# Two graph-convolution layers: part of each block's weights made directly behind the previous block's application, and several waits placed elsewhere

## The chip, the cores and the metric

The kernel runs on one core of a Trainium2 chip. The metric is the device time of one execution in microseconds (us). Smaller is better. The engines are named as in the profile: PE is TensorE's matrix multiplication, PEld its weight load, DVE is VectorE, ACT is ScalarE, POOL is GpSimd and SP is SyncE; the last two mostly start DMA transfers.

## What is computed

The input x has 8 batches of 2048 nodes with 64 features; adj is a 2048 x 2048 matrix. Two layers follow each other, each with a residual and a layer norm:

```
# layer 0: K = 3 supports I, A, 2A@A - I;  weights of each node from its embedding
w   = einsum('nd,dkio->nkio', embedding, weight);  b = einsum('nd,do->no', embedding, bias)
x_g = einsum('knm,bmc->bnkc', A_stack, x)
x   = layernorm(x + einsum('bnki,nkio->bno', x_g, w) + b)
# layer 1: the same with supports I, A, 2A@A - I and softmax(relu(E @ E.T))
x   = layernorm(x + einsum('bnki,nkio->bno', x_g, weights) + bias)
```

Every node has its own 64 x 64 weight matrix for each support. It is never held for all nodes: it is made for one block of 256 nodes, used there, and overwritten.

## The kernel before

**Stages.** The 2048 nodes are cut into 8 blocks of 256. The work is five phases of 8 stages, one stage per block: A0 (stages 0 to 7: layer 0, product of adj with x), B0 (8 to 15: layer 0, second product), A1 (16 to 23: layer 1, first product, and the row statistics of the softmax), Z1 (24 to 31: layer 1, product with the softmax matrix) and V1 (32 to 39: layer 1, second product of adj). Stages 26 to 31 work in pairs ("wide"). Block 0 of A0, B0, A1 and V1, block 1 of A0, and blocks 0 and 1 of Z1 use plain products; the other blocks use a seven-product (Strassen) scheme.

**The main product** of a stage is a Python generator that emits one matmul after another and reports its progress in units of the stage's length (64 for plain blocks, 56 for Strassen blocks). `put(n, place, job)` hangs a job on stage n at a place from 0 to 64, scaled to the length; as soon as the progress has reached the place, the job's instructions are emitted. `spread` puts several jobs at even distances. All instructions are kept in this program order on their engine's queue. So a place in this list is a position in every engine's queue, and an instruction that waits holds up all that stand behind it on its engine.

**The jobs that matter here:**

- `weights(g0, g1)` makes groups g0 to g1 - 1 of a block's node weights. There are 16 groups in A0, A1 and V1. A group is four matmuls `pw<-e,wst` (of 64 rows, two side by side) into one PSUM buffer, and one copy of 128 x 1024 values from it to `w`, on ACT or DVE. `cuts` says which groups go in one job. The jobs of stage n are hung on stage n + 1 (A0, A1) or on stage n itself (V1).
- `apply(c)` multiplies one quarter of a block with its weights (`po<-w,t`) into one PSUM buffer; DVE adds it into `acc` with four instructions. The four calls of a block follow each other in a "burst" on the next stage.
- `post` finishes a block of B0 or V1: the layer norm, in three parts (mean and squares; variance; scaling and store). For B0 the store goes to `x1d` in DRAM, and `load_x` brings it back as X for layer 1.
- `repeat` copies half of the transposed features `t` to the other half by a DMA (`t<-t`), which B0's applications need.
- `bias` makes a block's bias (`pb<-bst,e`) and adds it to x on DVE (`bx`).
- `load_e` loads a block's embedding into one of two tiles `e2` by POOL's queue (and in Z1 also `c`, the softmax constants).
- `numerators` and `scores` (`ps<-e,s`) make the softmax matrix, `scores_of_rows` (`pr`) its row statistics, `turn` (`pt`) transposes.

**Buffers.** `pw`, `po`, `pb`, `pt`, `ps` and `pr` all take the next one of three PSUM buffers of 4 KB per partition (pool `ps_big`, `bufs=3`); each waits until the tile three places ahead of it has been read out. The main products use two accumulators (`ps_acc`, `bufs=2`): the seven products p1, p4, p7, p2, p6, p5, p3 take them in turn, so p3 needs what p6 used.

The lines of the plan that are touched are 776 (`cuts`), 784 to 794 (B0), 818 (`bias`), 827 (`load` of `load_e` in Z1), and line 331 (which engine copies a group).

Of the kernel before, what the change touches and what calls it, by code (L numbers as in the profile page):

```python
# [24 lines left out]
SB = NB // P  # L25
# [4 lines left out]
V1 = C // 4  # L30
# [18 lines left out]
def two_graph_layers(ctx: ExitStack, tc: tile.TileContext, x, x_t, adj_b, adj_q, layers, out):  # L49
# [40 lines left out]
    def big(name):  # L90
        return ps_big.tile([P, 2, 512], F32, tag="big", name=name)

    def copy(i, dst, src):

        if i % 2:
            act.activation(dst, src, AF.Copy)
        else:
            dve.tensor_copy(dst, src)
# [42 lines left out]
    ps = big("pi")  # L141
# [120 lines left out]
    class Stage:  # L262
# [50 lines left out]
        def weights(self, g0, g1):  # L313
            if g0 == 0:
                self.w = w_room[:, 0:NB * self.units].rearrange("p (n o) -> p n o", n=NB)
            made = []
            for g in range(g0, g1):
                if g % 4 == 0:
                    self.ws = wst.next()
                ps = big("pw").rearrange("p h (v n) -> p h v n", n=NB)  # L320
                for i in range(2):
                    for h in range(2):
                        r = slice(64 * h, 64 * h + 64)
                        pe.matmul(ps[:, h, i, :], self.ws[r, 2 * (g % 4) + i, :], self.e2[r, :],
                                  start=True, stop=True)
                made.append(ps)
            if g1 == self.units // 4:
                wst.fill()
            for g, ps in zip(range(g0, g1), made):
                dst = self.w[:, :, 4 * g:4 * g + 4].rearrange("p n (v h) -> p n v h", h=2)  # L330
                copy(0 if g % (8 if self.phase == "A0" else 3) == 1 else 1, dst, ps.rearrange("p h v n -> p n v h"))


        def apply(self, c):
# [405 lines left out]
    def put(n, i, f, *args):  # L740
        plans[n].setdefault(i * stages[n].length / 64, []).append((f, args))

    def spread(n, first, last, jobs):
        for i, job in enumerate(jobs):
            put(n, first + (last - first) * i / max(len(jobs) - 1, 1), *job)
# [28 lines left out]
    for n, st in enumerate(stages):  # L774
        phase = st.phase
        cuts = (0, 3, 6, 9, 12, 14, 16) if st.units == C else (0, 3, 6, 8)
        weights = [(st.weights, *g) for g in zip(cuts, cuts[1:])]
        bursts = None
        if phase == "A0":
            for c in range(NJ // 4 if st.j == 1 else 0):  # L780
                put(n, 16 * c + 10, st.sums_of_a, c)
            spread(n + 1, 1, 31, weights)
            turned, bursts, posts = 33, (38, 38, 38, 38), (50,)
        elif phase == "B0":
            if st.j == 7:
                spread(n, 40, 60, weights)
                bursts, posts = (6, 6, 12, 12), ()
                put(n + 1, 26, st.load_x, range(SB))
                for k in range(6):
                    put(n + 1, (13 if k < 3 else 14) + 2 * k, st.post, k % 3, 8 - k // 3 * 8, 16 - k // 3 * 8)  # L790
            else:
                spread(n + 1, 3, 13, weights)
                bursts, posts = (19, 19, 29, 29), (38, 42, 48)
                put(n + 2, 5, st.load_x, range(SB))
        elif phase == "A1":
            spread(n + 1, 12, 36, weights)
            turned, bursts, posts = 4, (43, 43, 43, 43), (56,)
            for s, h, place in ((0, 0, 38), (0, 1, 40), (1, 0, 57), (1, 1, 60)):
                put(n, place, st.scores_of_rows, s, h)
            put(n, 41, st.statistics, 0)  # L800
            put(*((n, 62) if st.j else (n + 1, 6)), st.statistics, 1)
            put(n + 1, 24, st.store_c)
        elif phase == "V1":
            spread(n, (22 if st.j else 4), (62 if st.j < 7 else 52), weights)
            bursts, posts = (4, 4, 4, 4), (15, 19, 23)
            put(n, 20, st.load_z)
        if bursts and n + 1 < len(stages):
            if phase[0] == "A":
                put(n + 1, turned, st.turn, 1)
            for i, place in enumerate(bursts):  # L810
                put(n + 1, place, st.apply, i if phase == "A0" else i ^ 2)
            for k, place in enumerate(posts):
                put(n + 1, place, st.post, k)
        if n + 1 < len(stages):
            if n < 25 or n > 30:
                put(n, 44 if n < 23 else 37 if n < 25 else 4, stages[n + 1].load_e)
        if phase[0] == "A":
            put(*((1, 12) if n == 0 else (n, 28) if st.li == 0 else (n, 37)), st.bias)
            if st.li == 0:
                put(max(n, 1), 20 if n else 4, st.load_xt)  # L820
            else:
                put(n, 47 if st.j else 57, st.turn, 0, "x")
        if phase != "Z1":
            put(*((1, 26) if n == 0 else (n, 48 + 6 * st.li) if st.kk == 0 else (n, 30)), st.load_acc)
        elif st.wide:
            first, even, odd = (n - 2, (16, 24, 32), (40, 48, 56)) if n % 2 == 0 else (n - 2, (28, 36, 44), (4, 12, 20))
            load = (n - 2, 4) if n % 2 == 0 else (n - 3, 20)
            if n == 26:
                first, even, odd, load = 25, (4, 10, 18), (20, 26, 34), (24, 40)
            elif n == 27:  # L830
                first, even, odd, load = 25, (56, 61, 67), (42, 48, 54), (25, 33)
            put(*load, st.load_e)
            for t, places in enumerate((even, odd)):
                for i, place in enumerate(places):
                    at = (first, place) if place < 64 else (first + 1, place - 64)
                    put(*at, *((st.numerators, t, i) if i < 2 else (st.normalize, t)))
        else:
            st.p = [None] * 8
            for c in range(8):
                if c < 3:  # L840
                    put(n - 1, (50, 54, 62)[c] if n < 26 else 40 + 8 * c, st.scores, c)
                else:
                    put(n, 8 * (c - 3), st.scores, c)
# [71 lines left out]
```

## Time and profile before

| | |
|---|---|
| time, median of 3 runs | 1491.45 us (1489.88 to 1492.27) |
| the profiled execution: its own time | 1492.28 us |
| its span, first to last instruction | 1490.5 us |
| mean granted TensorE clock | 0.993 |
| PE busy, share of the span | 1453.0 us, 97% |
| DVE busy | 954.6 us, 64% |
| ACT busy | 474.1 us, 32% |
| POOL busy | 207.4 us, 14% |

The profile page has a line for each engine's busy time, the span in 40 slices, and the chain of work that ended last. The trace behind it can be asked for the instructions in order of time ("timeline"). A timeline line gives the start in us, the duration in us, the engine, the program line (nearly always that of a helper, L43), the operation with its tiles, how often it was repeated, and in square brackets the idle time before it and what ended it. The trace counts each fp32 matmul of the program as two instructions, and the `pw`, `pb`, `pr` and `ps` matmuls as one.

### The profile page before, as it was taken

To read this page: it belongs to the slowest core of one execution; us is meant where nothing else is said; L and a number is where in the kernel's file an instruction comes from. 1 tells how busy PE (TensorE), PEld (TensorE's weight loads), DVE (VectorE), ACT (ScalarE), POOL (GpSimd) and SP (SyncE) were. 2 spreads that over 40 slices of the span, in tenths; PEclk is the share of its full clock that TensorE was granted. 3 is DMA by queue.
4 is the path that set the end of the run, shared out by engine and by line. 5 is a ranking of instruction groups with operands and counts; after the bars stand their busy time and mean duration, and the time that the engine had idled before them with its cause. 6 is when DMAs were issued, how large, how long until landed. Compare 5 with 4: busy or idle time off the path is not lost.

```text
span 1490.5 us, 31130 instructions
## 1 busy us (share of the span) xinstructions
PE 1453.0 (97%) x13310; PEld 1182.8 (79%) x13310; DVE 954.6 (64%) x1614; ACT 474.1 (32%) x590; POOL 207.4 (14%) x343
## 2 busy tenths in 40 slices
PE   9899999999999999899999999999999999999996
PEld 4467777778989989467777777788888888888885
DVE  3876666637666666766666667567794466666665
ACT  1344444432211212064444444432120233333332
POOL 4222221210111111111011111101100000000100
PEclk9999999999999999999999999999999999999998
DMA  9788898884656666578777787212313656666551
GB/s 360 251 280 264 276 282 267 267 317 154 203 189 202 202 197 204 157 177 186 195 192 175 198 209 208 50 40 66 90 43 112 206 180 193 192 190 194 190 194 51
DMA packets 86730, 283.37 MB, mean 190 GB/s; under 512 B 14016, under 2 KB 18112, under 8 KB 84992
## 3 DMA queue, kind: packets, MB, share of 16 engines
q1 hardware_dynamic: 53600, 171.99, 38.5%
q0 software_dynamic: 27520, 95.76, 21.2%
q10 hardware_dynamic: 5472, 13.63, 2.9%
q8 instruction: 105, 1.72, 0.5%
q14 instruction: 33, 0.27, 0.1%
HBM read 216.28 MB, written 60.83 MB: 186 GB/s over the span
## 4 chain that ended last, share of the span: by engine, by line
PE 70%; issue 20%; DVE 3%; POOL 3%; DMA 3%; ACT 1%; POOLq 0%; ACTq 0%; DVEq 0%
PE p L43 40%; PE po L43 11%; PE pw L43 8%; PE pz L43 6%; PE pu L43 2%; PE pt L43 1%; DMA x<-in_x 1%; DVE w L43 1%; PE pr L43 1%; DVE acc L43 1%; PE ps L43 1%; POOL e L43 1%; POOL x1d L43 1%; DMA u<-in_w 1%; POOL t L43 1%
## 5 line engine op out<-in xcount | busy, mean ns | idle before, releaser
L43 ACT ACTIVATE w<-pw 128x1024 f32<-128x1024 f32 x328 | 318.5, 1021 | 391.6 <-PE pw L43 388.9
L43 DVE SCALAR_TENSOR_TENSOR acc<-po,mask,acc 128x256 f32<-128x256 f32 (+1 forms) x640 | 247.0, 426 | 82.7 <-PE po L43 70.0
L43 DVE COPY w<-pw 128x1024 f32<-128x1024 f32 x120 | 146.9, 1224 | 140.7 <-PE pw L43 139.4
L43 PE MATMUL p<-a,u 128*128 128x128 f32 x1792 | 219.4, 278 | 4.4 <-PE p L43 4.1
L43 PEld LDWEIGHTS p<-a,u 128*128 128x128 f32 x1792 | 206.6, 192 | 15.2 <-PE p L43 5.1
L43 PE MATMUL po<-w,t 128*32 128x256 f32 (+1 forms) x5120 | 206.1, 337 | 6.1 <-issue 5.0
L43 PE MATMUL p<-u,a 128*128 128x256 f32 x832 | 203.6, 387 | 0.0
L43 PEld LDWEIGHTS po<-w,t 128*32 128x32 f32 (+1 forms) x5120 | 125.9, 108 | 80.0 <-issue 14.0
L43 PEld LDWEIGHTS p<-u,a 128*128 128x128 f32 x832 | 152.0, 190 | 29.7 <-issue 5.4
L43 PE MATMUL p<-x,a 128*128 128x256 f32 x624 | 152.6, 385 | 0.0
L43 PE MATMUL pw<-e,wst 64*128 64x256 f32 x1728 | 146.0, 296 | 1.2 <-ACT w L43 1.1
L43 PEld LDWEIGHTS pw<-e,wst 64*128 64x128 f32 x1728 | 112.1, 184 | 41.8 <-issue 21.6
L43 PEld LDWEIGHTS p<-x,a 128*128 128x128 f32 x624 | 114.2, 190 | 19.0 <-issue 0.7
L43 PE MATMUL pu<-x,a 128*128 128x512 f32 x192 | 90.5, 617 | 3.6 <-DMA x<-x1d 2.1
L43 PE MATMUL p<-w,u 128*128 128x256 f32 x384 | 87.5, 384 | 0.0
L43 PE MATMUL p<-a,x 128*128 128x128 f32 x672 | 82.9, 278 | 0.0
L43 PE MATMUL p<-a,w 128*128 128x128 f32 x672 | 81.3, 277 | 0.0
L43 PEld LDWEIGHTS p<-w,u 128*128 128x128 f32 x384 | 73.2, 193 | 9.8
L43 PEld LDWEIGHTS p<-a,x 128*128 128x128 f32 x672 | 77.7, 192 | 2.8
L43 PEld LDWEIGHTS p<-a,w 128*128 128x128 f32 x672 | 77.3, 192 | 2.5 <-issue 1.4
L43 DVE TENSOR_TENSOR temps<-p,temps 128x256 f32<-128x256 f32 x108 | 43.1, 420 | 44.4 <-PE p L43 43.7
L43 PEld LDWEIGHTS pu<-x,a 128*128 128x128 f32 x192 | 35.5, 193 | 45.1 <-issue 36.1
(122 smaller groups left out, 1413.8 us busy)
## 6 DMA issues: line engine op xcount, KB each, us to landing
wst<-wd SPq DMA_DIRECT2D x108, 512.0 KB, 6.5
a<-in_adj_q SPq DMA_DIRECT2D x87, 512.0 KB, 5.2
a<-sd SPq DMA_DIRECT2D x84, 512.0 KB, 4.2
sd<-a POOLq DMA_DIRECT2D x24, 512.0 KB, 6.4
a<-in_adj_b SPq DMA_DIRECT2D x16, 512.0 KB, 6.5
bx<-bx POOLq DMA_DIRECT2D x32, 256.0 KB, 6.7
acc<-bx POOLq DMA_DIRECT2D x16, 512.0 KB, 6.1
pd<-acc POOLq DMA_DIRECT2D x16, 512.0 KB, 5.0
```

Of the source, the lines that this page charges most:

```text
L43: return self._tc.keep_in_program_order(f(*args, **kwargs))
```

## The change

The first group of weights of blocks 1 to 7 in A0, A1 and V1 is made directly behind the last call of the previous block's application (places 38, 43 and 4), and the other 15 groups follow in five jobs of three instead of the earlier six jobs for 16 groups. In A0 the copies that go to DVE are groups 2 and 10 instead of 1 and 9, and none for stage 0. The bias of stage 0 moves from stage 1, place 12, to stage 0, place 28. In B0 parts 1 and 2 of the norm move from places 42 and 48 to 46.5 and 50. The last application of layer 0 (block 7 of B0, in stage 16) moves from places 6 and 12 to 0 and 6, with its norm parts and `load_x` 6 places earlier. In Z1 the embedding loads of stages 28 to 31 move: 28 from (26, 4) to (25, 40), 29 from (26, 20) to (26, 8), 30 from (28, 4) to (27, 4), 31 from (28, 20) to (28, 8).

```diff
-                copy(0 if g % (8 if self.phase == "A0" else 3) == 1 else 1, dst, ps.rearrange("p h v n -> p n v h"))
+                copy(0 if self.n and g % (8 if self.phase == "A0" else 3) == (2 if self.phase == "A0" else 1) else 1, dst, ps.rearrange("p h v n -> p n v h"))
...
         cuts = (0, 3, 6, 9, 12, 14, 16) if st.units == C else (0, 3, 6, 8)
+        behind = {"A0": 38, "A1": 43, "V1": 4}.get(phase) if st.j else None
+        if behind:
+            put(n, behind, st.weights, 0, 1)
+            cuts = (1, 4, 7, 10, 13, 16)
         weights = [(st.weights, *g) for g in zip(cuts, cuts[1:])]
...
             if st.j == 7:
                 spread(n, 40, 60, weights)
-                bursts, posts = (6, 6, 12, 12), ()
-                put(n + 1, 26, st.load_x, range(SB))
+                bursts, posts = (0, 0, 6, 6), ()
+                put(n + 1, 20, st.load_x, range(SB))
                 for k in range(6):
-                    put(n + 1, (13 if k < 3 else 14) + 2 * k, st.post, k % 3, 8 - k // 3 * 8, 16 - k // 3 * 8)
+                    put(n + 1, (7 if k < 3 else 8) + 2 * k, st.post, k % 3, 8 - k // 3 * 8, 16 - k // 3 * 8)
             else:
                 spread(n + 1, 3, 13, weights)
-                bursts, posts = (19, 19, 29, 29), (38, 42, 48)
+                bursts, posts = (19, 19, 29, 29), (38, 46.5, 50)
...
-            put(*((1, 12) if n == 0 else (n, 28) if st.li == 0 else (n, 37)), st.bias)
+            put(*((n, 28) if st.li == 0 else (n, 37)), st.bias)
...
-            load = (n - 2, 4) if n % 2 == 0 else (n - 3, 20)
+            load = ((25, 40) if n == 28 else (n - 3, 4)) if n % 2 == 0 else (n - 3, 8)
```

## The prediction

> **What bounds the kernel now.** First the page: busy time, then the chain.
>
> ```profile
> PE 1453.0 (97%) x13310; PEld 1182.8 (79%) x13310; DVE 954.6 (64%) x1614; ACT 474.1 (32%) x590; POOL 207.4 (14%) x343
> ...
> PE 70%; issue 20%; DVE 3%; POOL 3%; DMA 3%; ACT 1%; POOLq 0%; ACTq 0%; DVEq 0%
> ```
>
> TensorE is the bound: every gap in its queue ends up in the time, and other engines count only where it waits for them. So I read its timeline for waits (idle time and its releaser in brackets).
>
> ```profile
> 40.22 0.72 PE L43 MATMUL pw<-e,wsplit 64*128 64x256 f32 x8 [1.36 <-DVE w L43]
> 47.01 0.51 PE L43 MATMUL pw<-e,wsplit 64*128 64x256 f32 x4 [2.41 <-DVE bx L43]
> ...
> 488.66 5.15 PE L43 MATMUL p<-a,u 128*128 128x128 f32 x44 [0.69 <-PE p L43]
> ...
> 602.24 2.01 PE L43 MATMUL po<-w,t 64*32 64x128 f32 x126 [1.12 <-DMA t<-t]
> ...
> 630.30 1.12 PE L43 MATMUL pu<-x,a 128*128 128x512 f32 x2 [1.97 <-DMA x<-x1d]
> ...
> 1016.42 0.71 PE L43 MATMUL ps<-e,s 128*128 128x256 f32 x4 [2.00 <-DMA e<-ed]
> 1071.98 0.71 PE L43 MATMUL ps<-e,s 128*128 128x256 f32 x4 [1.50 <-DMA e<-ed]
> ```
>
> Each stands where the change moves something. Then the windows view behind three of them (PEclk is the column before the DMA share):
>
> ```profile
> 632.00:636.00 4.00, 4.00 (x11) 2.01 (x10) 3.86 (x12) 1.84 (x2) 2.09 (x4) 0.57 0.47 164
> 1017.50:1021.50 4.00, 4.00 (x14) 3.18 (x12) 3.81 (x3) 1.53 (x2) 0.00 (x0) 0.57 0.04 14
> 48.00:51.50 3.50, 3.50 (x6) 1.10 (x4) 1.07 (x1) 0.58 (x1) 1.83 (x4) 0.57 1.02 290
> ```
>
> Each time the clock is halved for 3.41 us, so 1.7 us are lost. Start to start, matmuls of 128, 256 and 512 columns cost 112, 216 and 429 ns in the undisturbed streams; what exceeds this is the loss used below.
>
> [...]
>
> **The change, part by part.**
>
> *First group behind the application.* Weights jobs of 12 matmuls take 905 ns, of 8 665: 60 ns each and 181 fixed. The neighbouring products are 92 ns late before and 104 after: 377 ns per interruption. One interruption in each of 21 stages (7 each in A0, A1, V1) goes; in its place comes a change from `po` (128 x 32) to `pw` (64 x 128). No trace row shows it; bounds are 0 and the 270 ns (92 + 181) that `pw` costs out of a product. I take 200: gain about 0.17 us (0.1 to 0.37), x21 = **-3.6** (-2 to -7.7). The buffer it asks for was `po` number two's: DVE starts on A1's block at 709.28 and needs 7.89 / 4 = 1.97 us a tile, so 713.2, while TensorE asks at 714.3. No wait; A0 and V1 likewise have 1.0 us. ACT's copy (1.02 us) lies in idle ACT time: 9 us in A1 and V1, 17 us in A0.
>
> *The five jobs of three.* Each fills all three PSUM buffers, and whoever comes next waits for the first group's copy. In A1 that is the bias, one matmul behind the last job:
>
> ```profile
> 702.68 0.73 PE L43 MATMUL pw<-e,wst 64*128 64x256 f32 x8
> 703.34 0.70 PE L43 MATMUL p<-u,a 128*128 128x256 f32 x2
> 703.69 0.49 PE L43 MATMUL pb<-bst,e 128*128 128x64 f32 x2
> ```
>
> Now this job has groups 13, 14, 15, and 13 goes to DVE (13 modulo 3 is 1). Job start + 0.55 (from such jobs' first copies) + 1.22 copy + 0.06 = 1.83; `pb` asks at 0.905 + 0.35 = 1.25. Wait 0.58, in stages 18 to 23: **+3.5**. In A0 the transposes ask at 1.44 and ACT frees the buffer at 0.60 + 1.02 + 0.06 = 1.68: 0.24 in stages 2 to 7, **+1.4**. In stage 24 `ps` stands right behind a job: 1.83 - 0.905 = **+0.9**. V1 has nothing close behind.
>
> *B0's norm parts.* At 487.8 p3 waits for p6's buffer, because DVE runs the variance (1.22 us, and 1.18 waiting for ACT's squares) ahead of p6's sums. At 46.5 it comes after them (p6 ends at 40 of 56, place 45.7). Excess over cadence 0.80 to 0.87 us in stages 9 to 14: **-5.1**. Next latest: p5's sums, about 0.65 us ahead of their need.
>
> *Stage 0's bias.* At place 28 TensorE has done 28 rows of `pu`, at about 18.2 us, and meets `pb`, which needs the embedding:
>
> ```profile
> 14.75 20.01 PE L43 MATMUL pu<-x,a 128*128 128x512 f32 x46 [0.35 <-DMA x<-in_x]
> ...
> 17.78 1.16 POOL L43 DMA_DIRECT2D e<-ed x2
> ...
> DMA to landing us min/median/max: 5.6/5.7/6.0
> ```
>
> The second transfer starts at 18.36 and lands at 24.1: a wait of 5.9, then half clock, 1.7 (0.9 to 2.6). Behind it on DVE, `bx` pushes the splits 1.1 us, which TensorE no longer feels. POOL issues `bx` ahead of the next embedding (20.6 to about 27), needed only near 60. In stage 1 the waits go: 1.6 (copies all on ACT, 3 x 0.97 us per 3.5), 2.67 (`bx`), 1.66 of clock. **+1.7** (0.5 to 3).
>
> *Layer 0's last application.* TensorE gets to it at 598.05. `t<-t` is issued at 596.10 and landed 6.1 later, at 602.2. Before, six `pu` rows covered part. Now it waits 4.2, and 1.5 of clock follow. The second pair meets the second copy (599.40, landed 7.5 later) as before. Posts: DVE's start is unchanged, but the scaling is no longer behind a 2.02 us sum, so X lands at about 629.1; TensorE, 2.6 us of matmuls behind, asks at 631.6. Gone: 1.4, 2.1 and 1.7. 4.2 + 1.5 - 5.2 = **+0.6** (-1.5 to +3).
>
> *Z1's loads.* Stage 28's stood on POOL behind `zd<-t`, which waited for DVE until 1011.06. At (25, 40) it goes once stage 26's `c` is free, about 996; need 1014. Stage 30's gains a stage. Excesses 2.17 and 1.66, clock 1.7: **-5.5** (-3.8 without the clock). Stages 29 and 31 had no wait: nothing. POOL passes the loads ahead of stores needed a phase later.
>
> *Nothing:* groups 2 and 10 for 1 and 9 in A0 keep DVE's work the same.
>
> **Sum:** -3.6 + 3.5 + 1.4 + 0.9 - 5.1 + 1.7 + 0.6 - 5.5 = -6.1 against the profiled 1492.28 (span 1490.5 and 1.8 around it): 1486.2. That execution is 0.8 above the median[...]. I say 1486. A difference under 0.2% (3 us) can't be told from none.
>
> **Rivals.**
>
> *Less: no difference (16%).* [...]the group at 270 (+1.5), Z1's clock gain absent (+1.7): -0.9, 1491. [...]Against: all three must coincide.
>
> *More (13%).* The three-job waits (5.8 together) don't appear, because the copies start earlier than 0.55: -11.9, 1480. Against: start and copy were measured on many jobs.
>
> *Slower (12%).* The group behind the application waits for DVE. It asks 1.0 us after its buffer comes free. If DVE's drain is 1.0 + d late, 21 stages lose d each; from d = 0.43 (9.1 / 21) the kernel is over 0.2% slower; d = 0.7 gives 1501. For: in A0 DVE enters the burst straight from other work (144.56, a tenth late). Against: `po` shows no wait on DVE there. That the change doesn't do what it says is no rival: queue order follows the plan.
>
> Faster holds the rest: 72%, same 16, slower 12. The likeliest case alone is 1482 to 1490; for 8 in 10 I take 1479 to 1492.5, which adds the rivals' near ends.
>
> **To look for after:** a wait of about 6 us on `e<-ed` near 18 us; 4 us on `t<-t` near 600; `pw` x4 behind `po` without a wait; no p3 gaps in B0; 0.6 us before `pb` in A1; none at `ps` near 1010 and 1065. A `pw` wait behind `po`, or A1 without its `pb` wait, would make me wrong.

## The result and the profile after

The changed kernel took 1493.99 us (median; 1493.32 to 1494.92), the kernel before in the runs beside it 1490.66 (1488.69 to 1492.27): a ratio of 1.0023, 95% interval 1.0006 to 1.0041. The forecast was 1486.0 and faster; it became slower by about 3 us. The profiled executions lie closer together than the medians: 1492.28 before (at the top of its range) and 1493.32 after (at the bottom of its own), spans 1490.5 and 1491.6.

The page of the changed kernel, busy time and chain:

```profile
PE 1450.4 (97%) x13310; PEld 1185.0 (79%) x13310; DVE 953.4 (64%) x1612; ACT 476.9 (32%) x592; POOL 206.8 (14%) x343
...
PE 53%; DMA 1%; DVE 1%; issue 1%; ACT 1%; ACTq 0%
```

Nothing has changed hands: TensorE has the same work and is still the bound. (The second line's shares of the chain add up to only 57% of the span, so the chain is no guide here.) So again the waits in TensorE's timeline decide, here at the places that the prediction listed (the last column is the idle time before the line and what ended it):

```profile
25.11 0.61 PE L43 MATMUL pb<-bst,e 128*128 128x64 f32 x2 [6.95 <-DMA e<-ed]
43.87 0.97 PE L43 MATMUL pw<-e,wsplit 64*128 64x256 f32 x12
...
485.78 3.74 PE L43 MATMUL p<-a,w 128*128 128x128 f32 x32
489.35 5.08 PE L43 MATMUL p<-a,u 128*128 128x128 f32 x44
...
603.12 3.41 PE L43 MATMUL po<-w,t 64*32 64x128 f32 x126 [5.31 <-DMA t<-t]
...
644.12 1.97 PE L43 MATMUL pt<-ident,u 128*128 128x128 f32 x8 [2.62 <-ACT u L43]
...
1013.97 0.82 PE L43 MATMUL ps<-e,s 128*128 128x256 f32 x4
1073.91 0.83 PE L43 MATMUL ps<-e,s 128*128 128x256 f32 x4
```

Stage 1's weights, p3 in B0 and Z1's `ps` have lost their brackets, as forecast. The embedding and `t<-t` are waited for, as forecast, but for longer. The wait of `pt` on ACT is new and was not forecast. The windows view shows the clock (0.50 in the column before the DMA share) at half rate behind all three waits:

```profile
22.50:29.00 6.50, 3.89 (x6) 1.94 (x7) 3.17 (x5) 1.28 (x1) 2.23 (x4) 0.50 1.05 380
602.80:606.00 3.20, 2.88 (x112) 2.88 (x119) 0.83 (x4) 0.00 (x0) 0.00 (x0) 0.50 1.01 206
643.80:647.00 3.20, 2.88 (x11) 2.71 (x12) 0.00 (x0) 1.13 (x3) 0.00 (x0) 0.50 0.63 194
```

**Where the time went.** Each block's application is a burst of `po` on TensorE. The differences between the starts of these bursts cut the span into pieces that can be compared between all kernels. The columns: *start* is the time of the first burst; *A0* and *A1* run from their first block's burst to their last; *B0* over its first seven blocks; *16* from B0's seventh burst to A1's first, so layer 0's last application and what follows; *Z1* from A1's last block's burst to V1's first; *V1* from there to the second half of the very last application. The piece between A0 and B0 is 29.5 us in every kernel, and what follows the last column 19.0 to 19.4. Each row is one execution.

| kernel (us, profiled execution) | start | A0 | B0 | 16 | A1 | Z1 | V1 |
|---|---|---|---|---|---|---|---|
| before | 63.5 | 273.6 | 205.3 | 94.0 | 292.8 | 243.3 | 269.1 |
| changed | 66.5 | 275.2 | 200.0 | 98.4 | 296.9 | 237.5 | 268.5 |
| stage 16 put back | 66.3 | 275.2 | 199.9 | 99.0 | 295.9 | 237.5 | 268.1 |
| stage 0's bias at 48 | 57.3 | 275.2 | 200.0 | 101.1 | 297.5 | 237.5 | 267.8 |
| other bias places | 67.5 | 274.4 | 199.6 | 99.7 | 293.2 | 237.5 | 267.8 |
| old cuts | 66.3 | 273.6 | 199.9 | 99.9 | 292.9 | 237.5 | 269.1 |
| late refill | 67.5 | 276.8 | 200.6 | 97.0 | 296.4 | 237.5 | 267.8 |
| before + norm parts | 63.8 | 273.6 | 199.9 | 98.9 | 292.9 | 241.4 | 269.1 |
| before + norm parts + late refill | 62.2 | 273.6 | 199.3 | 94.2 | 292.8 | 241.9 | 269.1 |
| before + Z1's loads | 61.9 | 273.6 | 204.5 | 94.7 | 293.2 | 237.5 | 269.1 |
| combined | 60.3 | 273.6 | 200.0 | 92.6 | 292.8 | 237.5 | 268.2 |

Forecast against measured, by piece (the forecast is the sum of the prediction's own terms): start +1.7 against +3.0; A0 +0.2 against +1.5; B0 -5.1 against -5.3; stage 16 +0.6 against +4.4; A1 +3.2 against +4.0; Z1 -5.5 against -5.8; V1 -1.2 against -0.6. That is -6.1 against +1.3. Half of the miss, 3.8 of 7.4, is stage 16.

### The profile page after: what moved, and what is told of

It reads as the page before. It is cut to its first block, busy times and chain, and to the rows that moved or that the text cites. A ratio compares the mean times of both kernels' runs of the same rounds, so it can differ in the third digit from the quotient of the medians.

```text
span 1491.6 us, 31148 instructions
## 1 busy us (share of the span) xinstructions
PE 1450.4 (97%) x13310; PEld 1185.0 (79%) x13310; DVE 953.4 (64%) x1612; ACT 476.9 (32%) x592; POOL 206.8 (14%) x343
## 4 chain that ended last, share of the span: by engine, by line
PE 53%; DMA 1%; DVE 1%; issue 1%; ACT 1%; ACTq 0%
PE p L43 32%; PE po L43 7%; PE pz L43 6%; PE pw L43 5%; DMA wst<-wd 1%; PE ps L43 1%; PE pt L43 1%; PE pr L43 1%; DVE w L43 1%; DVE acc L43 0%; PE pb L43 0%; ACT row L43 0%; ACT t L43 0%; ACT sq L43 0%; ACT w L43 0%
## 5 line engine op out<-in xcount | busy, mean ns | idle before, releaser
L43 ACT ACTIVATE sq<-acc 128x1024 f32<-128x1024 f32 (+2 forms) x19 | 17.5, 922 | 166.5 <-DVE acc L43 153.9
```

Source lines behind the costliest of these rows:

```text
L43: return self._tc.keep_in_program_order(f(*args, **kwargs))
```

## The experiments

The kernels are measured against the kernel before, run beside them on the same chip; times are medians.

**1. Stage 16 put back.** The obvious suspect first.

```diff
-                bursts, posts = (0, 0, 6, 6), ()
-                put(n + 1, 20, st.load_x, range(SB))
+                bursts, posts = (6, 6, 12, 12), ()
+                put(n + 1, 26, st.load_x, range(SB))
-                    put(n + 1, (7 if k < 3 else 8) + 2 * k, st.post, k % 3, 8 - k // 3 * 8, 16 - k // 3 * 8)
+                    put(n + 1, (13 if k < 3 else 14) + 2 * k, st.post, k % 3, 8 - k // 3 * 8, 16 - k // 3 * 8)
```

> The changed kernel with layer 0's last application (stage 16) at its old places: bursts (6, 6, 12, 12), posts at 13/14, load_x at 26; all else as changed. Theory (the early application cost TensorE 5.3 us of waiting on t<-t and, by emptying the queue, uncovered the chain DVE sums - statistics - ACT table load - u copy, 2.6 us more, plus two halved clock stretches): the stretch from stage 15's to stage 17's application is about 4.5 us shorter than in the changed kernel's profile (offset there from -0.8 to +3.7), with po waiting 1.1 on t<-t and pu 2.0 on X again, and no wait of pt on ACT. Whole time -4 to -4.5 against the changed kernel. Rival (only the landing time of that one DMA was unlucky, 7.3 instead of 6.1, and the rest would have come out equal): the stretch is 1.2 us shorter at most.

Measured: 1493.95 us, ratio 1.0019 (1.0009 to 1.0029). Stage 16 took 99.0 us, not less than the 98.4 with the change. The theory fell: with the application back at its old place TensorE still waited 3.5 us for `t<-t` (1.1 before), 2.8 for X and 2.0 for ACT's `u`. Something else in the change had made `t<-t` late: 8.1 us from its issue to the application, 6.1 before.

**2. Stage 0's bias at place 48.**

```diff
-            put(*((n, 28) if st.li == 0 else (n, 37)), st.bias)
+            put(*((0, 48) if n == 0 else (n, 28) if st.li == 0 else (n, 37)), st.bias)
```

> The changed kernel with only stage 0's bias moved from place 28 to place 48 of stage 0, where its embedding has landed (25.0 us in the changed kernel's profile; TensorE gets to place 48 near 27). Theory (the wait of 6.95 us on e<-ed and the 1.8 us of half clock are lost only because of the place): no wait in stage 0 and none back in stage 1, since bx (1.3 us) ends long before the first weights; stage 0 is 8.5 to 8.8 us shorter than in the changed kernel. Rival (the embedding's arrival or bx's place in DVE's queue, between the splits of 2.5 us, costs it again a little later, as pw<-DVE bx near 45): only 3 to 5 us shorter.

Measured: 1486.38 us, ratio 0.9972 (0.9959 to 0.9985). The first application came at 57.3 instead of 66.5, 9.2 us earlier, and 6.2 earlier than in the kernel before. `pb` stood at 26.24 with no wait, and the first weights at 34.68 without one. The theory held; the place alone cost it.

**3. Other bias places in A0 and A1.**

```diff
-            put(*((n, 28) if st.li == 0 else (n, 37)), st.bias)
+            put(*((0, 28) if n == 0 else (n, 26) if st.li == 0 else (n, 33)), st.bias)
```

> The changed kernel with only the biases of stages 1 to 7 and 16 to 23 moved: A0 from place 28 to 26, A1 from 37 to 33, so that pb and its bx are not next to the last job of three groups. Theory (one cause for both losses: with three groups in a row all three PSUM buffers are taken, and the bias's buffer is one of the three): A0's last jobs are 905 instead of 1410 to 1460 ns long, 0.47 less in each of stages 2 to 7; in A1 the 0.39 ahead of pb goes in stages 18 to 23, with at most 0.07 of it back ahead of pr. Sum -4.6 to -5.2. Rival (the copies as such are late, since more of them go behind one another on DVE, whatever stands next): the wait moves to pr in A1 and to pt in A0, sum 0 to -1.

Measured: 1490.41 us, ratio 0.9993 (0.9981 to 1.0006). A1's piece lost 3.6 us, A0's only 0.8. The changed kernel first, in A0: the timeline of a stage's end.

```profile
178.13 0.49 PE L43 MATMUL pb<-bst,e 128*128 128x64 f32 x2
...
180.90 0.51 PE L43 MATMUL pw<-e,wst 64*128 64x256 f32 x4 [0.23 <-DVE bx L43]
181.33 0.70 PE L43 MATMUL p<-x,a 128*128 128x256 f32 x2
181.87 0.82 PE L43 MATMUL pt<-ident,u 128*128 128x128 f32 x6
```

The job's third group asks for the buffer of the bias, three places ahead of it, and DVE reads that only at 179.47 to 180.75. From the job's start at 179.93 to the next product matmul it is 1.40 us instead of 0.905. The transposes then follow 0.54 us behind the product matmul, as usual. With the bias moved:

```profile
180.78 0.97 PE L43 MATMUL pw<-e,wst 64*128 64x256 f32 x12
181.68 0.70 PE L43 MATMUL p<-x,a 128*128 128x256 f32 x2
182.46 0.76 PE L43 MATMUL pt<-ident,u 128*128 128x128 f32 x5
```

The job is 0.90 us long again, and now the transposes come 0.78 behind the product matmul: 0.24 late, the very wait that the prediction had for this place. It had been there all along, behind a longer one. So in A0 the rival (the wait moves to `pt`) was right by half; in A1 the theory held.

**4. Old cuts.** The lines of `behind` and `cuts` taken out; groups 1 and 9 on DVE in A0, none in stage 0.

> The changed kernel without the group behind the application: old cuts (0, 3, 6, 9, 12, 14, 16), groups 1 and 9 on DVE in A0 (none in stage 0); all else as changed. Theory (the group behind the application saves 0.19 us per stage, and its jobs of three lose 0.47 in A0 and 0.49 in A1 at the bias): against the changed kernel's profile stages 2 to 7 -0.28 each, A1's -0.29 each, stage 24 -0.8, V1's +0.19 each: sum about -1.7 -1.7 -0.8 +1.3 = -2.9. Rival (the group behind the application is itself late, so that its removal brings more in every phase, V1 too): V1's stages shorter as well, sum -4 and beyond.

Measured: 1489.69 us, ratio 0.9984 (0.9971 to 0.9997). The steps of A0 fell by 0.28 and those of A1 by 0.29 each, stage 24 by 0.8, and V1's rose by 0.17 to 0.21: the theory, stage by stage. A0, A1 and V1 together gave 4.9 instead of 2.9, as two waits in A1 for the refill of `wst` (stages 18 and 23, 0.5 and 1.0) and a gap of 0.6 in V1 went as well; the whole execution shows 3.8, since stage 16 took 1.4 more in this one. V1 shows the gain of the group behind the application directly. In A0 and A1 it is what is left once the waits behind the jobs of three are taken off, and these waits cost more than it brings.

**5. Late refill.** What made `t<-t` late? In the trace two transfers stand close together: POOL's `t<-t`, and SP's refill of `wst` that stage 15's last weights job releases. The DMA issues of the kernel before, of the changed kernel, and of the kernel before with the norm parts alone (number 6), in this order (SPq is SP's queue):

```profile
596.10 0.53 POOL L43 DMA_DIRECT2D t<-t  x1 [0.86 <-DVE t L43]
596.52 0.33 SPq L43 DMA_DIRECT2D wst<-wd  x1
```

```profile
595.79 0.33 SPq L43 DMA_DIRECT2D wst<-wd  x1
595.82 0.53 POOL L43 DMA_DIRECT2D t<-t  x1 [0.85 <-DVE t L43]
```

```profile
591.58 0.33 SPq L43 DMA_DIRECT2D wst<-wd  x1
591.59 0.53 POOL L43 DMA_DIRECT2D t<-t  x1 [0.86 <-DVE t L43]
```

Before, the copy was issued 0.42 us ahead of the refill; since, just behind it. The edit moves the refill back:

```diff
-                spread(n, 40, 60, weights)
+                spread(n, 40, 50, weights[:2])
+                put(n, 63, *weights[2])
```

> The changed kernel with only the last weights job of stage 15 moved from place 60 to 63 (about 0.8 us later), so that the refill of wst (512 KB on SP's queue) that it releases is issued behind the first t<-t instead of 0.03 us ahead of it. In the kernel before, t<-t was issued 0.42 us ahead of that refill, and the application followed 6.1 us after its issue; in the changed kernel and the four kernels built on it the refill went 0.02 to 0.17 us ahead, and it took 7.3 to 9.0 us. Theory (the norm parts' move takes p3's stalls out of B0, TensorE ends its weights job earlier against DVE, and so the refill goes ahead of t<-t through the same DMA engines): the application follows 6.0 to 6.4 us after the issue, the wait at po is 4.2 to 4.6. Rival (chance, or the store x1d<-acc 2.1 us ahead of t<-t in every kernel): 7.3 us or more, as in the other five.

Measured: 1491.66 us, ratio 0.9994 (0.9985 to 1.0004). The application followed 5.4 us after the issue, and `po` waited 2.3 us for the copy, behind 1.0 for a weights copy that the later job itself delays. Stage 16 took 97.0 us, where the changed kernel took 98.4 and the four built on it without this edit 99.0 to 101.1.

**6. The norm parts alone**, on the kernel before: `posts` (38, 46.5, 50) instead of (38, 42, 48).

> The kernel before with one part of the change: B0's norm parts at (38, 46.5, 50). Theory: up to stage 15's application -5.3 as forecast (waits of p3 gone), and then a price that the forecast did not see: the wst refill goes ahead of t<-t, which lands 7.3 to 9 us after its issue instead of 6.1. The six pu rows cover 2.8 of it, so the wait at po grows from 1.1 to 2.5 to 4.2 us, and an idle time over 2 us can halve the clock (1.7 more); X and the rest follow that chain. Whole time against before: -5.3 +1.5 to +4.5, that is -1 to -4. Rival (the landing time has nothing to do with the norm parts): wait at po 1.0 to 1.5, whole time -5.3.

Measured: 1490.29 us, ratio 0.9989 (0.9977 to 1.0000). B0 gave 5.3 us and stage 16 took 4.9 back. Its timeline:

```profile
595.79 0.40 PE L43 MATMUL po<-w,t 64*32 64x128 f32 x2
599.64 3.66 PE L43 MATMUL po<-w,t 64*32 64x128 f32 x126 [3.45 <-DMA t<-t]
```

The application stands at its old place, and yet waits 3.45 us instead of 1.12. The 126 matmuls took 3.66 us instead of 2.01 and the six of `pu` behind them 3.62 instead of 2.84, 2.4 us more together: the times of a halved clock, as in the changed kernel, where the same 126 took 3.41 at a clock of 0.50.

The DMA view shows how the two queues shared the 16 DMA engines. In the fourth us after the issue of `t<-t`, SP's queue took 87% of their time in the changed kernel and POOL's queue 11%; in the kernel before it was 38% for SP and 46% for POOL.

**7. The norm parts with the late refill**, on the kernel before: the edits of 6 and 5 together.

> The kernel before with two edits: B0's norm parts at (38, 46.5, 50), and stage 15's last weights job at 63 instead of 60. With the norm parts alone t<-t went 0.01 us behind the refill of wst, the application followed 8.0 us after its issue, and stage 16 gave back 4.9 of the 5.3 us. Theory (order of t<-t and the refill on the DMA engines): the application follows 5.4 to 6.5 us after t<-t's issue, as in the three runs with the late job; po waits 0 to 1.2 us without a halved clock, stages 15 and 16 together take at most 94.5 us (94.0 before, 98.9 with the norm parts alone), and the whole is -4 to -6 against before. Rival (it is the kernel around it, not the order): 98 us again and -0.5 to -2.

Measured: 1485.21 us, ratio 0.9956 (0.9940 to 0.9973). Stage 16 took 94.2 us.

```profile
589.14 0.53 POOL L43 DMA_DIRECT2D t<-t  x1 [0.85 <-DVE t L43]
590.46 0.33 SPq L43 DMA_DIRECT2D wst<-wd  x1
...
594.79 2.01 PE L43 MATMUL po<-w,t 64*32 64x128 f32 x126 [1.07 <-DMA t<-t]
```

The copy is ahead of the refill again, lands in time, and the wait is 1.07. One place of one job, and the same norm parts give 7 us instead of 2. So what experiment 1 left open is the refill: issued behind the copy, here by 1.3 us, it no longer delays it. (Z1's column in numbers 6 and 7 is 1.5 to 1.9 lower than before although nothing was edited there. Before, the clock was halved for 3.41 us behind a wait for the embedding of 2.00, which cost 1.7; here the longest of these waits were 1.9 and 2.0. That the clock was not halved behind them would fit the column, but was not shown.)

**8. Z1's loads alone**, on the kernel before: only the `load` line.

> The kernel before with one part of the change: Z1's embedding loads. Theory: the waits of ps on e<-ed near 1016 and 1072 (2.2 and 1.7 above cadence) and the halved clock behind the first (1.7) go, -5.5 to -5.8 in Z1, nothing elsewhere. Rival (the loads, now ahead of zd and other stores on POOL's queue, hold those up, or e comes too early and waits for its tile's release): a new wait in Z1 and -3 or less.

Measured: 1489.22 us, ratio 0.9978 (0.9962 to 0.9993). Z1 gave 5.80 us, as in the changed kernel, and no wait took their place. The profiled execution was the fastest of this kernel; by the medians the whole is 3.9 faster.

**9. Combined.** The parts that gained, without those that lost. Stage 0's bias at (0, 48), the late refill, old cuts in A0 and A1 and `behind` for V1 alone, norm parts and Z1's loads as changed, and a new order in stage 16:

```diff
-        behind = {"A0": 38, "A1": 43, "V1": 4}.get(phase) if st.j else None
+        behind = {"V1": 4}.get(phase) if st.j else None
...
-                bursts, posts = (0, 0, 6, 6), ()
-                put(n + 1, 20, st.load_x, range(SB))
+                bursts, posts = (9, 9, 14, 14), ()
+                put(n + 1, 23, st.load_x, range(SB))
-                    put(n + 1, (7 if k < 3 else 8) + 2 * k, st.post, k % 3, 8 - k // 3 * 8, 16 - k // 3 * 8)
+                    put(n + 1, 15 + k, st.post, k % 3, 8 - k // 3 * 8, 16 - k // 3 * 8)
...
-        put(16, 24 + 4 * i, sums["A1"].make, i, 0, 7)
-        put(16, 50, sums["A1"].make, i, 7, 8)
+        put(16, 24 + 4 * i if i < 2 else 42, sums["A1"].make, i, 0, 7)
+        put(17, 2, sums["A1"].make, i, 7, 8)
```

> The parts of the change that gained, without those that lost: B0's norm parts and Z1's loads as changed; the group behind the application in V1 only (A0 and A1 with the old cuts); stage 0's bias at (0, 48), with stage 0's groups all on ACT; stage 15's last weights job at 63; and stage 16 in a new order: bursts (9, 9, 14, 14), norm parts at 15 to 20, load_x at 23, two of the four A1 sums for blocks 0 to 6 behind the first row statistics (place 42 instead of 32 and 36), and the sums' last eighth at (17, 2) instead of (16, 50). Expected against before: start -5.8, B0 -5.3, Z1 -5.8, V1 -1.3, stage 16 -3 to -6 (no wait at po over 1 us, no halved clock; pt's wait on ACT gone because the statistics no longer stand behind 10 us of sums): about -21 to -24, near 1468. Rival (stage 16's chain of t<-t, application, norm and x1d is one length whatever the order, so its waits only move to pu<-X or pt): stage 16 gives 0 to -1, near 1472.

Measured: 1474.97 us, ratio 0.9883 (0.9863 to 0.9904): faster than both kernels, by less than expected. The start gave 3.2 instead of 5.8, as `pt` in stage 1 waited 1.5 us for that stage's bias and `po` behind it another 0.8. Stage 16 gave 1.4: `po` waited 0.36 and `pt` no longer, but TensorE now reaches X 2.63 us too early, and the clock is halved behind that wait (4.58 us for six matmuls that took 2.84 behind `po` in the kernel before):

```profile
594.36 2.01 PE L43 MATMUL po<-w,t 64*32 64x128 f32 x126 [0.36 <-DMA t<-t]
620.89 4.58 PE L43 MATMUL pu<-x,a 128*128 128x512 f32 x6 [2.63 <-DMA x<-x1d]
```

The rival was nearer the mark there.

**10. Combined, with the sums as before.** It tells what `pt`'s wait on ACT hangs on.

> As the combined kernel, but all four A1 sums at their old places (16, 24 to 36) and the last eighth at (16, 50). It tells apart what pt<-ACT u hangs on. Theory (ten us of sums on DVE hold up the row statistics, these the exponentials on ACT, these the copy of u): pt waits 4 to 7 us on ACT's u copy (2.6 in the changed kernel, where TensorE came 5 to 7 us later), and the whole is 3 to 6 us slower than the combined kernel. Rival (pt's wait came from the clock or from X): within 1 us of the combined kernel.

Measured: 1476.56 us, ratio 0.9895 (0.9874 to 0.9916). From the second pair of applications to A1's first burst it took 60.8 us instead of 57.7. The theory holds for the stretch, but not in its detail: DVE's sums delayed first the bias's read, so that `pr` waited 1.51 us, and `pt` waited only 1.15 on ACT. Of the 3 us the whole shows 1.6, and the two intervals overlap; in the profiled execution the start, among others, was 0.9 shorter.

**11. Combined 2.** Stage 1's bias at 22 instead of 28, and X's last block loaded half by half.

> The combined kernel with two more edits. The bias of stage 1 goes from place 28 to 22, ahead of the second of the sums of a on DVE, which in the combined kernel waited 4.5 us for a store's landing and held up bx, so that pt waited 1.5 us and po another 0.8. And X's last block comes back in two loads, each issued behind its own half's store, not both behind the second. Expected: stage 0 and 1 together 2.5 to 3 shorter than in the combined kernel's profile (60.3 to about 57.5 at the first application); the wait of pu on X (2.63, with 1.7 of halved clock) less by 0 to 1 us, since the half that comes last still lands at about the same time. Whole: 1471 to 1473. Rival (the first application hangs on ACT's copies and not on bx): stage 1 unchanged, 1474 to 1475.

Measured: 1476.08 us, ratio 0.9889 (0.9876 to 0.9903), beside the first combined kernel's 0.9883: no gain in the whole. The start did fall to 57.9, as expected, but the wait for X stayed at 2.9 us, and A1 showed two waits of 0.7 and 0.6 for the refill of `wst` that the first one did not have.

**12. The group behind the application in all three phases**, on combined 2, with the biases at 26 and 33 and A0's transposes at 35.

> As combined 2, but with the group behind the application in A0 and A1 as well, as the change has it, and what made it lose there moved away: biases at 26 (A0) and 33 (A1) as in the run with other bias places, and A0's transposes at 35 instead of 33, because in that run they had taken over a wait of 0.25 us. Expected against combined 2: A0's steps 38.63 to 38.5, A1's 41.39 to 41.29, stage 24 +0.8 (ps behind the last job of three): sum -0.6, that is the same within the error. Rival (the transposes at 35 meet the application or the copies of t come late): A0's steps 38.8 or more, sum over +0.5.

Measured: 1482.24 us, ratio 0.9929 (0.9916 to 0.9941), so 6 us slower than combined 2. A0's steps were 38.80, as the rival said; A1's piece took 299.2 us. There four jobs waited 0.34 to 0.94 us for the refill of `wst`, one 1.10 for ACT's copy, and one product 1.00 for a piece of adj (`a<-in_adj_q`). In stage 33, V1's second, a gap of 1.70 us has no releaser in the trace. Why the refills are late here and not in experiment 3, with the same cuts and biases in A1, stays open.

## Why the prediction was wrong, step by step

**First group behind the application: right, a little small.** In all 21 places the first `pw` starts 309 ns behind the last `po`, and no wait shows. The gain was 0.19 us a stage in V1 and, once the waits of the next step are taken out, 0.22 in A0 (0.50 - 0.28) and 0.28 in A1 (0.57 - 0.29); the forecast was 0.17. The rival that made the kernel slower (this group waits for DVE) didn't happen. V1's sum came out at -0.6, since one gap of 0.6 us without a releaser fell into stage 33.

**The five jobs of three: right in A1, the wrong wait in A0.** In A1 `pb` came 602 ns behind its product matmul instead of 28, so it waits 0.57; the forecast was 0.58. In stage 24 `ps` is 0.92 late; forecast 0.9:

```profile
790.67 0.70 PE L43 MATMUL p<-u,a 128*128 128x256 f32 x2
791.59 0.41 PE L43 MATMUL pb<-bst,e 128*128 128x64 f32 x2 [0.22 <-DVE w L43]
...
912.99 0.50 PE L43 MATMUL pw<-e,wst 64*128 64x256 f32 x4 [0.71 <-DMA wst<-wd]
...
955.29 0.51 PE L43 MATMUL ps<-e,s 128*128 128x256 f32 x2 [0.85 <-DVE w L43]
```

The line at 912.99 was not foreseen: in two stages a refill of `wst` came late, 1.5 us together. In A0 the prediction looked at who comes behind the job, and not at whose buffer the job's third group needs. That is the bias's, and it cost 0.50 a stage where the prediction had 0.24 for the transposes. Both waits exist (experiment 3); the first hides the second. This is 1.3 of the miss.

**B0's norm parts: right for B0, and half of what it does.** B0 gave 5.3 us for 5.1. But TensorE now ends stage 15's last weights job some 0.4 us earlier against DVE. The refill of 512 KB that this job releases therefore goes ahead of `t<-t` and no longer behind it. The prediction followed the DMAs that the norm parts issue, and not the transfers of others whose order they upset.

**Layer 0's last application: the step that failed.** Forecast +0.6, measured +4.4. Two terms failed: that DVE's start is unchanged, and that 5.2 us of waits are gone.

What ends the stage is a chain that nothing in the forecast followed: DVE's adding of the second pair of applications, its norm parts, then 10 us of sums, then the row statistics, then ACT's table load and exponentials, and behind these ACT's copy of `u`, which the transposes `pt` need. In the kernel before, the adding starts at 608.17, the copy ends at 641.24, and `pt` starts 0.05 us later. That is 0.32 us after the matmul ahead of it, where these transposes elsewhere follow after 0.22: TensorE waited for the copy already there, though too short a time to be listed.

```profile
608.17 4.23 DVE L43 SCALAR_TENSOR_TENSOR acc<-po,mask,acc 128x128 f32<-128x128 f32 x16 [0.51 <-PE po L43]
...
640.64 0.60 ACT L43 ACTIVATE u<-pu 128x512 f32<-128x512 f32 x1
641.29 1.09 PE L43 MATMUL pt<-ident,u 128*128 128x128 f32 x8
```

In the changed kernel:

```profile
610.44 4.23 DVE L43 SCALAR_TENSOR_TENSOR acc<-po,mask,acc 128x128 f32<-128x128 f32 x16 [1.05 <-PE po L43]
...
637.00 1.28 ACT L43 ACT_TABLE_LOAD   x1 [14.84 <-DVE low L43]
...
642.18 1.26 ACT L43 ACTIVATE t<-pt 64x512 f32<-64x512 f32 x2 [1.52 <-issue]
643.46 0.60 ACT L43 ACTIVATE u<-pu 128x512 f32<-128x512 f32 x1
```

From DVE's start to the end of the copy it is 33.0 to 33.6 us in the kernel before, in the changed one and in experiments 1 to 8, and in all of them `pt` starts 0.05 us behind the copy. So the wait for X and the halved clock behind it (2.1 and 1.7 of the 5.2) only filled time that this chain needed anyway. They did go, and `pt`'s wait of 2.62 and half a clock for 3.4 us came in their place. Experiments 1, 6 and 7 show it without the move: in 1 and 6 the `pu` matmuls behind the wait for X ran at full rate (two in 1.13 us, six in 2.84), and in all three `pt` waited 2.0 to 2.3 us.

Against B0's seventh burst, DVE's start came 3.0 us later. Half of that, 1.5, follows from the forecast's own terms: the first pair at 602.2, 2.0 of matmuls, 1.5 of halved clock and 2.8 of `pu` rows put the second pair at 608.5, and in the kernel before it stood at 606.96. The other half is mostly "landed 6.1 later": that landing time, read from the kernel before, held only for the order of transfers before. Behind the refill it took 7.3 in the profiled execution and 8.1 to 9.0 in the four others; `po` waited 5.3 to 7.0 us in those with the application at 0, for a forecast of 4.2. The rest of the 4.4 is 0.6 for a longer chain and 0.8 behind `pt`.

What the move costs by itself depends on the order. With the refill ahead, the old place is no better (99.0 in experiment 1, against 98.4). With the copy ahead, the old place takes 94.2 (experiment 7) and the new one 97.0 (experiment 5, which differs from it in other parts too): 2.8 for a forecast of 0.6.

**Stage 0's bias: right mechanism, two sizes off.** The forecast had the second transfer of the embedding start at 18.36 and land at 24.1; POOL issued the pair only from 18.54 on, with its own queue ahead of it slower, and it landed near 25.0. So TensorE waited 6.95 us instead of 5.9, and the halved clock cost 2.1 (of 6.8 us, the 4.2 behind the wait) instead of 1.7. The forecast's range for the clock, 0.9 to 2.6, and the 2.0 us that the rival "no difference" needs beside its other two terms were the author's estimate: each of the three halvings looked at in the kernel before lasted 3.41 us and cost 1.7. The waits of stage 1 went as forecast.

**Z1's loads: right**, with the clock's share, 5.8 for 5.5. That share may not be in every execution: Z1 took 1.5 to 1.9 less than before in experiments 6 and 7, where nothing of it was edited.

**The sum.** By piece and rounded, up to V1's last application: +3.8 for stage 16, +1.3 for the start, +1.3 for A0, +0.8 for A1, +0.6 for V1, less 0.5 in B0 and Z1: 7.4 us between the forecast -6.1 and the profiles' +1.3. The medians lie 2 us further apart than the profiles. The profiled execution of before was above its median, and that of the changed kernel had the shortest wait for `t<-t` of the four with this code (5.3 against 6.1 to 7.0); how much of the 2 us each explains was not measured.

## To carry to other kernels

A landing time read from a trace belongs to the order in which transfers were issued there (here 6.1 us ahead of the refill, 7.3 to 9.0 behind it): where an edit shifts one engine by some tenths of a us against another, look which transfers change places, above all a large refill and a small copy that is waited for. When buffers go round in a ring, ask for every group both who comes three places behind it and whose buffer it needs itself; in A0 the longer wait, 0.50 us, hid the other, 0.24. And when a stall goes, follow every other chain that ends at the same place and see how much slack it has; here it had none (`pt` started 0.05 us behind ACT's copy already before), and the stall had been its cover.

## What the runs showed of the hardware

- With two DMAs of different queues, issued 0.01 to 1.3 us apart, the order counted: `t<-t` (256 KB) took 7.3 to 9.0 us to the application behind a refill of 512 KB issued 0.01 to 0.17 us ahead of it (six kernels), and 5.4 to 6.6 ahead of it, even with only 0.40 to 0.42 us between them (five kernels).
- The halving of the clock was not told by the idle time alone: waits of 1.97, 2.00 and 2.41 us (before), of 2.62 (changed) and of 2.63 (combined) brought it, and one of 1.50 (before) and waits for X of 2.57 (experiment 6), 2.83 (experiment 1) and 2.90 us (combined 2) did not. Nor was its length: it was 3.41 us with waits of 1.97 to 2.62 and with one of 5.31, and 6.8 with one of 6.95. With one of 3.45 (experiment 6) the matmuls took 2.4 us longer, where half rate for 3.41 us costs 1.7.
- An instruction that waited held up those behind it on its engine: in the changed kernel TensorE stood still for the 6.95 us in which `pb` waited for the embedding; with `pb` at place 48 (experiment 2) it ran 16 matmuls of `pu` from 19.77 to 26.24 without a wait.
